# A selective-scan kernel: b made in quads of states, one more product on GpSimd, a second buffer for the inputs

## The chip, the cores and the metric

The kernel runs on one core of one Trainium2 chip. The metric is device time in microseconds (us) of one execution; lower is better. The core has five engines with instruction queues of their own, each worked off in order: TensorE (PE, matrix products), VectorE (DVE), ScalarE (ACT), GpSimd (POOL) and SyncE (SP), which here only issues transfers between DRAM and the core's memory.

## The reference

The input has shape (2, 96, 128, 128). Two layers follow one another, and only the first half of layer 0 is touched by the change: a normalization over the 96 channels, then a selective scan (Mamba) in four directions over the 16,384 positions (rows, rows backwards, columns, columns backwards), fused by one matrix.

```
xz = x @ in_w.T;  xc, z = split(xz)            # 192 channels each
xc = silu(causal_conv4(xc) + conv_b)
dt_raw, B, C = split(xc @ xproj_w.T)           # 6, 16, 16
dt = softplus(dt_raw @ dt_w.T + dt_b)
h[t] = exp(dt[t] * A) * h[t-1] + dt[t] * B[t] * xc[t]   # per channel and state
y[t] = sum over the 16 states of h[t] * C[t],  then + D * xc[t]
out = (y * silu(z)) @ outp_w.T                 # then the fuse matrix over the 4 directions
```

After it come two small feed-forward layers with 8-bit rounding and a 3x3 depthwise convolution; they are not changed.

## The kernel before, in words

For each of the two images three stages run one after the other: `normalize` writes the normalized image to DRAM once in rows (xnr) and once in columns (xnc); `mamba` does the scan; `ffn_and_conv` does the rest.

`mamba` handles two directions at once: 2 x 192 = 384 channels are three groups g = 0, 1, 2 of 128 partitions. Time is cut into 32 tiles of T = 512 positions; with two pairs of directions that makes 64 steps an image. A step has 24 units, each a group g and a pair of states s, s+1 (s = 0, 2, ..., 14); unit number = 8g + s/2. For each unit:

- `decay` (ScalarE) makes da = exp(dt * A), two rows of 512, in PSUM (three buffers).
- `b_part` (GpSimd) multiplies dtu = dt * xc into the row of B that a transfer has spread over all 128 partitions, 128 x 1024, in place (line 345); a small addition on column 0 brings in the state from the step before (line 347), in every step but the first of a pair of directions.
- `scan` (VectorE, line 357) runs the recurrence over 512 positions, once for each state, in place over da.
- VectorE multiplies h by the spread row of C (line 431, "the product"); TensorE adds the products of all states into y by matrix products with the identity (`sums`, line 361).
- For the units in `BY_POOL`, (0, 4) and (1, 4), that is units 2 and 10, GpSimd makes the product instead (`by_pool`, line 364); the scan then writes over b. `by_pool` is put into the order one unit later, its sum three units later.

B and C rows are fetched by SyncE for four states at a time, 1 MB each once spread (`row_tile`, line 341); B has four buffers (row0), C three (row1). A buffer of C is free again when TensorE has summed it. `fetch` asks for B six units ahead and for C four units ahead, both from even units.

The next step's preparation (`prologue`) is interleaved with the units: input projection and convolution as matrix products (`conv`, three of them, for g = 1, 0, 2, at units 1, 3, 5), SiLU on ScalarE (`silu`, which loads an activation table before and after), B, C and dt rows, softplus with three additions on GpSimd (`dt_q`, `dt_log`, `dt_sum`, lines 295, 298, 301) and dtu (`dt_u`, line 305). `load` fetches the two input tiles xa and xb (T + 3 columns each) two units before the step in which they are used.

The order on every engine is that in which the code issues the instructions; a table `todo` holds, for each unit and each half of it (0: before the scans, 1: after), what is to be issued there. The loop over units k:

```
for k in range(total + 6):
    ...
    if k % 2 == 0:
        fetch(k + 2 * B_AHEAD, 0, B_AHEAD, bs)
    feed(k + AHEAD)
    issue(k, 0)
    ... scan(0), behind(k - 1), feed_decay(k + AHEAD), scan(1)
    if k % 2 == 0:
        fetch(k + 2 * C_AHEAD, 1, C_AHEAD, cs)
    issue(k, 1)
```

`behind(k - 1)` issues the product of the unit before and its sums, so unit k's two scans stand around the product of unit k - 1. At a group's first unit it also issues the gating of the finished group (`gated`, line 368).

Of the kernel before, what the change touches and what calls it, by code (L numbers as in the profile page):

```python
# [10 lines left out]
F32 = mybir.dt.float32  # L11
# [4 lines left out]
ALU = mybir.AluOpType  # L16
# [7 lines left out]
T = 512  # L24
# [8 lines left out]
B_AHEAD = 3  # L33
C_AHEAD = 2
AHEAD = 2
BY_POOL = ((0, 4), (1, 4))
BCO = 32
NBC = 4 * S

# [2 lines left out]
def tile_metaformer(ctx: ExitStack, tc: tile.TileContext, a: dict, out: bass.AP):  # L42
    nc = tc.nc
# [135 lines left out]
    def mamba(acc, xnr, xnc):  # L179

        with ExitStack() as st:
            pool = lambda n, bufs, **kw: st.enter_context(tc.tile_pool(name=n, bufs=bufs, **kw))
            io, one, two, gen = pool("io", 1), pool("one", 1), pool("two", 2), pool("gen", 4)
            ps_w, ps_y, ps_m = (pool(n, k, space=PSUM) for n, k in (("ps_w", 3), ("ps_y", 1), ("ps_m", 1)))
            rows_d = pool("rows_d", 3, space=DRAM)

# [1 line left out]
            enter = one.tile([128, NG, S], F32, name="enter")  # L188
# [18 lines left out]
            def prologue(pi, i, d):  # L207
# [19 lines left out]
                def conv_out(g):  # L227
                    if g == 1:
                        d["xc"] = two.tile([128, NG, T], F32, name="xc")
                    t = mixed("xc") if g == 1 else d["xc"][:, g, :]  # L230
                    nc.scalar.activation(t, d["ps"], AF.Identity, bias=convb[:, pi, g : g + 1])  # L231
# [4 lines left out]
                def gate_out(g):  # L236
                    if g == 1:
                        d["sz"] = two.tile([128, NG, T], F32, name="sz")
                    nc.scalar.copy(mixed("sz") if g == 1 else d["sz"][:, g, :], d["ps"])

                def mixed(name):
                    d["mix", name] = one.tile([128, T], F32, name=f"mix_{name}")
                    return d["mix", name]

                def mix(name):
# [89 lines left out]
            def row_tile(d, g, s, k, ahead):  # L335

                t = gen.tile([128, 4, T], F32, name=f"row{k}", bufs=ahead + 1)

                src = d["bcd"][k, s // 4] if g == 1 else d["bcd"][k, s // 4, g // 2 : g // 2 + 1]
                n = src.shape[0]  # L340
                nc.sync.dma_start(t, src[None].broadcast_to((128 // n, n, 4, T)))
                return t

            def b_part(i, d, g, s, b):
                nc.gpsimd.tensor_tensor(b, d["dtu"][g][:, None, :].broadcast_to((128, 2, T)), b, ALU.mult)  # L345
                if i > 0:
                    nc.gpsimd.tensor_tensor(b[:, :, 0], b[:, :, 0], enter[:, g, s : s + 2], ALU.add)  # L347

            def decay(pi, d, g, s):

# [5 lines left out]
            def scan(j, da, b, h):  # L356
                nc.vector.tensor_tensor_scan(h[:, j, :], da[:, j, :], b[:, j, :], 0.0, ALU.mult, ALU.add)  # L357
# [29 lines left out]
            steps = [(pi, i) for pi in range(2) for i in range(NT)]  # L387
            units = [(g, s) for g in range(NG) for s in range(0, S, 2)]
            nu = len(units)
            total = nu * len(steps)  # L390
            state = [{} for _ in steps]
            todo = {}

            def later(k, where, f, *args):
                todo.setdefault((k, where), []).append(partial(f, *args))

            def issue(k, where):
                for f in todo.pop((k, where), ()):
                    f()

            for k, where, f in prologue(*steps[0], state[0]):
                if k < nu:
                    f()
                else:
                    later(k - nu, where, f)
            bs, cs, das, hs = {}, {}, {}, {}

            def fetch(k, n, ahead, m):
                if k < total:
                    t = row_tile(state[k // nu], *units[k % nu], n, ahead)  # L410
                    m[k], m[k + 1] = t[:, 0:2, :], t[:, 2:4, :]

            def feed(k):
                if k < total:
                    n = k // nu
                    b_part(steps[n][1], state[n], *units[k % nu], bs[k])

            def feed_decay(k):
                if k < total:
                    n = k // nu  # L420
                    das[k] = decay(steps[n][0], state[n], *units[k % nu])
# [3 lines left out]
            def behind(k):  # L425

                n, u = divmod(k, nu)
                (pi, i), d, (g, s) = steps[n], state[n], units[u]
                h, c = hs.pop(k), cs.pop(k)
                if (g, s) not in BY_POOL:  # L430
                    nc.vector.tensor_tensor(c, h, c, ALU.mult)  # L431
                nc.scalar.copy(hst[:, g, s : s + 2], h[:, :, T - 1])  # L432
                if s == 0:
                    if k > 0:
                        pn, pu = divmod(k - 1, nu)
                        gated(steps[pn][0], state[pn], units[pu][0], ys.pop(k - 1))
                    y = ps_y.tile([128, T], F32, name="y")
                    nc.tensor.matmul(y, dmat[:, pi, g, :], d["xc"][:, g, :], start=True, stop=False)  # L438
                else:
                    y = ys.pop(k - 1)  # L440
                ys[k] = y
                if (g, s) in BY_POOL:
                    later(k + 1, 1, by_pool, h, c)
                    later(k + 3, 1, sums, s, y, c)
                else:
                    sums(s, y, c)
                if k == total - 1:
                    gated(pi, d, g, y)
                if s == S - 2 and g > 0:
                    later(k + 3, 0, project, pi, i, d, g)  # L450
                    later(k + 3, 1, collect, pi, d, g)

            for m, (n, ahead) in ((bs, (0, B_AHEAD)), (cs, (1, C_AHEAD))):
                for k in range(ahead):
                    fetch(2 * k, n, ahead, m)
            for k in range(AHEAD):
                feed(k)
                feed_decay(k)
            for k in range(total + 6):
                n, u = divmod(k, nu)  # L460

                ahead = 1 if k == 0 else n + 2 if u == nu - 2 else len(steps)
                if ahead < len(steps):
                    for m, where, f in prologue(*steps[ahead], state[ahead]):
                        later(max(k, (ahead - 1) * nu + m), where, f)
                if k % 2 == 0:
                    fetch(k + 2 * B_AHEAD, 0, B_AHEAD, bs)
                feed(k + AHEAD)
                issue(k, 0)
                if k < total:  # L470
                    (g, s) = units[u]
                    da, b = das.pop(k), bs.pop(k)
                    hs[k] = b if (g, s) in BY_POOL else da
                    scan(0, da, b, hs[k])
                if 0 < k <= total:
                    behind(k - 1)
                feed_decay(k + AHEAD)
                if k < total:
                    scan(1, da, b, hs[k])
# [3 lines that stand above are left out]
# [102 lines left out]
    for b in range(NB):  # L585
        xnr = dpool.tile([C, L], F32, name="xnr")
        xnc = dpool.tile([C, L], F32, name="xnc")
        normalize(b, acc, xnr, xnc)
        mamba(acc, xnr, xnc)
        ffn_and_conv(b, acc)  # L590
# [71 lines left out]
```

## Time and profile before

| | before |
|---|---|
| device time, median of 3 | 12191.46 us (12177.44 to 12192.11) |
| profiled span | 12199.4 us |
| VectorE busy | 10961.9 us, 90% |
| TensorE busy | 10593.4 us, 87% |
| GpSimd busy | 10388.1 us, 85% |
| ScalarE busy | 8592.7 us, 70% |
| granted TensorE clock | 0.975 of full |

The scan stage takes from about 145 to 5530 us and again from about 6230 to 11620 us of the span; `normalize` and `ffn_and_conv` take the rest. Within the scan stage VectorE is busy 96% and GpSimd 95% (for example 482.5 and 477.6 us of the 500 between 1000 and 1500 us), and the transfers move some 313 GB/s. Busy time is the union of the recorded durations, and two instructions of VectorE overlap in the records by about 0.09 us: what counts for a sum is the distance from one start to the next, 1.12 us for a scan whose mean duration is 1.215. A group's row reads: line, engine, operation, what it writes and reads, shape, count, then busy time and mean of one in ns, then idle time before it and what ended it.

### The profile page before, as it was taken

The page shows a single profiled execution, that of the slowest core. Times are in us where ns is not written, and L with a number is a line of the kernel's source. Part 1 is how long each engine was busy: PE and PEld are TensorE (multiplying, and loading weights), DVE is VectorE, ACT ScalarE, POOL GpSimd, SP SyncE. Part 2 cuts the span into 40 slices and gives each one's busy share as a digit, 9 for nine tenths or more (in the row PEclk, how much of TensorE's full clock was granted, in tenths as well). Part 3 has the DMA queues.
Part 4 walks back from the last instruction along what each step waited for, and adds up shares of the span by engine and source line. Part 5 has one row for each costly group of instructions (what it writes and reads, how often), then busy time and mean ns, then how long its engine had stood idle before and what let it go on. Part 6 is the DMA issues. An engine that isn't in the chain of part 4 may idle for free. (4 is left out here: it accounts for less than half of the span.)

```text
span 12199.4 us, 100157 instructions
## 1 busy us (share of the span) xinstructions
PE 10593.4 (87%) x24208; PEld 4009.0 (33%) x24208; DVE 10961.9 (90%) x10624; ACT 8592.7 (70%) x15110; POOL 10388.1 (85%) x8360
## 2 busy tenths in 40 slices
PE   7888888888888888888978888888888888888889
PEld 2333333333333333333323333333333333333333
DVE  5999999999999999995469999999999999999954
ACT  6777777777777777765567777777777777777655
POOL 4999999999999999991159999999999999999911
PEclk8999999999999999999989999999999999999999
DMA  6887888888878878871068888878877878878700
GB/s 237 310 321 306 312 319 312 314 318 313 315 307 311 319 304 316 314 307 43 26 231 311 310 315 312 320 312 312 320 303 311 315 312 313 310 305 317 305 32 13
DMA packets 539204, 3417.36 MB, mean 280 GB/s; under 512 B 67276, under 2 KB 68396, under 8 KB 140696
## 3 DMA queue, kind: packets, MB, share of 16 engines
q1 hardware_dynamic: 538616, 3410.94, 72.5%
q8 instruction: 195, 3.19, 0.1%
q14 instruction: 393, 3.22, 0.1%
HBM read 3289.04 MB, written 54.53 MB: 274 GB/s over the span
## 5 line engine op out<-in xcount | busy, mean ns | idle before, releaser
L345 POOL TENSOR_TENSOR row<-dtu,row 128x1024 f32<-128x1024 f32 x3072 | 7235.6, 2356 | 262.2 <-DMA row<-bcd 212.3
L357 DVE TENSOR_TENSOR_SCAN da<-da,row 128x512 f32<-128x512 f32 x5632 | 6649.6, 1215 | 509.8 <-POOL row L347 166.1
L361 PE MATMUL y<-row,ident 128*128 128x512 f32 x12288 | 5956.1, 618 | 1135.8 <-DVE row L431 1131.4
L353 ACT ACTIVATE da<-dt,amat 128x512 f32<-128x512 f32 x6144 | 4249.9, 692 | 286.4 <-DVE row L357 99.3
L361 PEld LDWEIGHTS y<-row,ident 128*128 128x128 f32 x12288 | 2265.7, 193 | 4646.6 <-issue 2284.6
L431 DVE TENSOR_TENSOR row<-da,row 128x1024 f32<-128x1024 f32 x2816 | 3395.9, 1206 | 3.2 <-DMA row<-bcd 3.1
L432 ACT COPY hst<-da 128x2 f32<-128x2 f32 x2816 | 435.4, 155 | 1450.9 <-DVE row L431 1436.5
L204 PE MATMUL misc<-xa,inx 96*64 96x512 f32 (+1 forms) x2048 | 950.5, 607 | 133.1 <-DMA xa<-xnr 97.5
L556 POOL TENSOR_TENSOR acc<-acc,y 96x512 f32<-96x512 f32 x128 | 147.6, 1153 | 987.0 <-DVE y L555 972.6
L204 PE MATMUL misc<-xb,inx 96*64 96x512 f32 (+1 forms) x2048 | 949.7, 607 | 1.6 <-ACT xc L231 1.6
L347 POOL TENSOR_TENSOR row<-row,enter 128x2 f32<-128x2 f32 x2976 | 577.4, 194 | 233.4
L357 DVE TENSOR_TENSOR_SCAN row<-da,row 128x512 f32<-128x512 f32 x512 | 617.0, 1205 | 0.0
L364 POOL TENSOR_TENSOR row<-row,row 128x1024 f32<-128x1024 f32 x256 | 602.7, 2354 | 1.2 <-issue 0.6
L568 PE MATMUL pc<-pad,kw 96*96 96x512 f32 x1152 | 566.8, 593 | 0.0
L438 PE MATMUL y<-xc,dmat 128*128 128x512 f32 x768 | 432.1, 645 | 145.8 <-DVE sz L368 145.8
L295 POOL TENSOR_TENSOR q<-e,q 128x512 f32<-128x512 f32 x384 | 487.3, 1269 | 76.6 <-ACT q L292 71.5
L231 ACT ACTIVATE xc<-misc,convb 128x512 f32<-128x512 f32 x256 | 175.9, 687 | 525.8 <-PE misc L204 525.8
L204 PEld LDWEIGHTS misc<-xa,inx 96*64 96x64 f32 (+1 forms) x2048 | 326.8, 165 | 643.3 <-issue 470.1
L301 POOL TENSOR_TENSOR dt<-dt,ln 128x512 f32<-128x512 f32 x384 | 488.2, 1271 | 30.1
L298 POOL TENSOR_TENSOR ln<-ln,q 128x512 f32<-128x512 f32 x384 | 488.3, 1272 | 0.2
L305 POOL TENSOR_TENSOR dtu<-dt,xc 128x512 f32<-128x512 f32 x384 | 487.9, 1271 | 0.2
L378 PE MATMUL misc<-sz,gmat 128*96 128x512 f32 x1024 | 483.5, 594 | 0.0
(81 smaller groups left out, 9124.5 us busy)
## 6 DMA issues: line engine op xcount, KB each, us to landing
row<-bcd SPq DMA_DIRECT2D x3072, 1024.0 KB, 7.0
xc<-mix_xc SPq DMA_DIRECT2D x256, 128.0 KB, 5.3
sz<-mix_sz SPq DMA_DIRECT2D x256, 128.0 KB, 5.4
xa<-xnr SPq DMA_DIRECT2D x124, 193.1 KB, 5.3
xb<-xnc SPq DMA_DIRECT2D x124, 193.1 KB, 5.5
bcd<-rows SPq DMA_DIRECT2D x128, 128.0 KB, 6.5
acc<-in_x_dram SPq DMA_DIRECT2D x16, 768.0 KB, 8.6
xnr<-xn SPq DMA_DIRECT2D x16, 768.0 KB, 4.3
```

What stands on the lines that cost most here:

```text
L204: nc.tensor.matmul(ps[rows, :], w(PAIRS[pi][d], k, lo, hi), src[d][:, k : k + T], **se)
L298: nc.gpsimd.tensor_tensor(d["ln"], d["ln"], d["q"], ALU.add)
L301: nc.gpsimd.tensor_tensor(d["dt"][g], d["dt"][g], d["ln"], ALU.add)
L305: nc.gpsimd.tensor_tensor(dtu, d["dt"][g], d["xc"][:, g, :], ALU.mult)
L345: nc.gpsimd.tensor_tensor(b, d["dtu"][g][:, None, :].broadcast_to((128, 2, T)), b, ALU.mult)
L347: nc.gpsimd.tensor_tensor(b[:, :, 0], b[:, :, 0], enter[:, g, s : s + 2], ALU.add)
L353: nc.scalar.activation(da[:, j, :], d["dt"][g], AF.Exp, scale=amat[:, pi, g, s + j : s + j + 1])
L357: nc.vector.tensor_tensor_scan(h[:, j, :], da[:, j, :], b[:, j, :], 0.0, ALU.mult, ALU.add)
L361: nc.tensor.matmul(y, ident, c[:, j, :], start=False, stop=s + j == S - 1)
L364: nc.gpsimd.tensor_tensor(c, h, c, ALU.mult)
L431: nc.vector.tensor_tensor(c, h, c, ALU.mult)
L568: nc.tensor.matmul(pc, kw[:, t, :], rows, start=t == 0, stop=t == 8)
```

## The change

The change has four parts. GpSimd makes b for four states in one instruction of 128 x 2048 instead of two of 128 x 1024, and adds the entering state for four states at once; this is meant to save instructions on GpSimd. The room goes to a third product by GpSimd, (2, 4), which is unit 18; this takes a product from VectorE. The input tiles xa and xb get a second buffer; to make room in memory, the two tiles that hold xc and z of the mixed group before they are rearranged share one buffer. The preparation of step 1 is issued before the first fetches of rows and not in unit 0; for all later steps the preparation is registered at the same unit as before.

```diff
-BY_POOL = ((0, 4), (1, 4))
+BY_POOL = ((0, 4), (1, 4), (2, 4))
...
-            io, one, two, gen = pool("io", 1), pool("one", 1), pool("two", 2), pool("gen", 4)
+            io, one, two, gen = pool("io", 2), pool("one", 1), pool("two", 2), pool("gen", 4)
...
-                    d["mix", name] = one.tile([128, T], F32, name=f"mix_{name}")
+                    d["mix", name] = one.tile([128, T], F32, name="mix")
...
-                nc.gpsimd.tensor_tensor(b, d["dtu"][g][:, None, :].broadcast_to((128, 2, T)), b, ALU.mult)
+                nc.gpsimd.tensor_tensor(b, d["dtu"][g][:, None, :].broadcast_to((128, 4, T)), b, ALU.mult)
                 if i > 0:
-                    nc.gpsimd.tensor_tensor(b[:, :, 0], b[:, :, 0], enter[:, g, s : s + 2], ALU.add)
+                    nc.gpsimd.tensor_tensor(b[:, :, 0], b[:, :, 0], enter[:, g, s : s + 4], ALU.add)
...
+            def prepare(n):
+                if n < len(steps):
+                    for m, where, f in prologue(*steps[n], state[n]):
+                        k = (n - 1) * nu + m
+                        if k < 0:
+                            f()
+                        else:
+                            later(k, where, f)
+
+            prepare(1)
...
                     m[k], m[k + 1] = t[:, 0:2, :], t[:, 2:4, :]
+                    if n == 0:
+                        quads[k] = t
...
-                    b_part(steps[n][1], state[n], *units[k % nu], bs[k])
+                    b_part(steps[n][1], state[n], *units[k % nu], quads.pop(k))
...
+            feed(0)
             for k in range(AHEAD):
-                feed(k)
                 feed_decay(k)
...
-                ahead = 1 if k == 0 else n + 2 if u == nu - 2 else len(steps)
-                if ahead < len(steps):
-                    for m, where, f in prologue(*steps[ahead], state[ahead]):
-                        later(max(k, (ahead - 1) * nu + m), where, f)
+                if u == nu - 2:
+                    prepare(n + 2)
                 if k % 2 == 0:
                     fetch(k + 2 * B_AHEAD, 0, B_AHEAD, bs)
-                feed(k + AHEAD)
+                    feed(k + AHEAD)
```

GpSimd's order after the change, from unit 12's quad on, as the program has it: quad 12, product 10, quad 14, entering, quad 16, softplus of the next step's first group up to its sum, quad 18, dtu, quad 20, softplus of the second group up to its sum, product 18, quad 22, dtu, entering, quad 0 of the next step, dt_q, quad 2, dt_log, dt_sum, dtu, quad 4, product 2, quad 6, entering, quad 8, quad 10.

More of the change, by code (lines that the diff above doesn't have):

```diff
@@ L405, in mamba @@
                     later(k - nu, where, f)
-            bs, cs, das, hs = {}, {}, {}, {}
+            def prepare(n):
[7 more added lines that the diff above has]
+            prepare(1)
+            bs, cs, das, hs, quads = {}, {}, {}, {}, {}
             def fetch(k, n, ahead, m):
```

## The prediction

> **What bounds the kernel now.** I read the page first (shares, costliest groups), then the timeline of each engine over one step of the scan stage, then the list of waits, SyncE's own included. A step (512 columns of both directions) has 24 units, numbered 0 to 23, unit = 8g + s/2.
>
> ```profile
> PE 10593.4 (87%) x24208; PEld 4009.0 (33%) x24208; DVE 10961.9 (90%) x10624; ACT 8592.7 (70%) x15110; POOL 10388.1 (85%) x8360
> L345 POOL TENSOR_TENSOR row<-dtu,row 128x1024 f32<-128x1024 f32 x3072 | 7235.6, 2356 | 262.2 <-DMA row<-bcd 212.3
> L364 POOL TENSOR_TENSOR row<-row,row 128x1024 f32<-128x1024 f32 x256 | 602.7, 2354 | 1.2 <-issue 0.6
> L301 POOL TENSOR_TENSOR dt<-dt,ln 128x512 f32<-128x512 f32 x384 | 488.2, 1271 | 30.1
> ```
>
> Totals don't decide. Per step VectorE has 48 scans and 22 products at a pitch of 1.12 us (start to start) and 3 gatings at 0.60: 80.3 us. GpSimd has 24 b at 2.585 (2.36 + 0.08 before the small addition + 0.145 for it), 2 products at 2.33, three softplus chains of 5.03 and 3 x 0.18: 82.3. Yet a step takes 83.2 in half of the cases and 84.05 on average (end of the last product to the next such end, in the timeline, the 124 steps after the first of each batch). So I asked which chain closes the step. VectorE around one step (start, duration, [wait]):
>
> ```profile
> 2005.05 1.21 DVE L431 TENSOR_TENSOR row<-da,row 128x1024 f32<-128x1024 f32 x1
> ...
> 2036.45 1.23 DVE L357 TENSOR_TENSOR_SCAN da<-da,row 128x512 f32<-128x512 f32 x1 [0.68 <-ACT hst L432]
> 2037.59 1.21 DVE L431 TENSOR_TENSOR row<-da,row 128x1024 f32<-128x1024 f32 x1
> ...
> 2088.26 1.21 DVE L431 TENSOR_TENSOR row<-da,row 128x1024 f32<-128x1024 f32 x1
> ```
>
> The first and last are unit 23's product; call its end P (2006.26). The 0.68 is the wait before unit 9; from there to the next P (2089.47) VectorE has no gap. TensorE and ScalarE fill the stretch before it:
>
> ```profile
> 2006.31 1.98 PE L361 MATMUL y<-row,ident 128*128 128x512 f32 x4 [1.38 <-DVE row L431]
> 2008.23 0.64 PE L204 MATMUL misc<-xa,inx 96*64 96x512 f32 x1
> ...
> 2024.80 3.60 PE L204 MATMUL misc<-xb,inx 96*128 96x512 f32 x8
> 2028.24 8.75 PE L361 MATMUL y<-row,ident 128*128 128x512 f32 x20
> ```
> ```profile
> 2028.44 0.69 ACT L231 ACTIVATE xc<-misc,convb 128x512 f32<-128x512 f32 x1 [1.43 <-PE misc L204]
> ...
> 2030.65 1.28 ACT L251 ACT_TABLE_LOAD   x1
> 2031.94 1.48 ACT L251 ACTIVATE xc<-xc 128x1536 f32<-128x1536 f32 x1
> 2033.44 1.28 ACT L252 ACT_TABLE_LOAD   x1
> ...
> 2034.93 1.42 ACT L353 ACTIVATE da<-dt,amat 128x512 f32<-128x512 f32 x2
> ```
>
> TensorE sums unit 23, then runs without a gap through the next step's three convolutions; ScalarE takes the last one, does the SiLU with its two table loads, then the decay of unit 9, and VectorE starts unit 9 at P+30.19. This loop (TensorE, ScalarE, VectorE) is the 83.2. Where the step is longer, the convolution mostly began late, waiting for xa or xb.
>
> GpSimd stands in a second loop, just short of binding:
>
> ```profile
> 2038.33 0.20 POOL L347 TENSOR_TENSOR row<-row,enter 128x2 f32<-128x2 f32 x1
> 2039.26 2.35 POOL L345 TENSOR_TENSOR row<-dtu,row 128x1024 f32<-128x1024 f32 x1 [0.74 <-DMA row<-bcd]
> ```
> ```profile
> POOL row L345 <- DMA row<-bcd: 212.3, 104, 6.6
> SPq L341 <- PE y L361: 5297.7, 1518, 15.5
> ```
>
> SyncE issues in order, and mostly waits for TensorE to free a C buffer. C of units 8, 9 takes the buffer of units 2, 3, and unit 2 is one of GpSimd's products, summed late: in the middle of the x20 above, at 2031.8. SyncE issues at 2031.87, B of unit 12 behind it at P+26.2, landing at P+33.4. So GpSimd starts unit 12 at P+33.54 (median; mean 34.12). From there it has no gap until b of unit 23 is ready, 43.76 later; VectorE needs 5.69 from scan 23 to P. Together 33.54 + 49.45 = 83.0: 0.2 under the other loop, and in the slower steps over it.
>
> **What the Trainium skill says.** "GPSIMD Engine Reference", 3.1, gives 4497 ns for a two-input fp32 operation of 2048 elements. The trace agrees in slope: 1271 ns at 512 and 2356 at 1024 make 1085 per 512, hence 4.53 us at 2048, with 0.19 saved against two halves. The same page, 8, says that GpSimd shares its SBUF interfaces with VectorE when that has two SBUF inputs; here L345 stays between 2337 and 2380 ns beside a full VectorE, so I add nothing. "DMA: Bandwidth & Descriptors", Anatomy of one DMA, fits 2.0 us + bytes/436e3, an estimate of 4.4 us for 1 MB; here the median is 7.0, since transfers queue. "Perfetto Trace Analysis", Optimizing Scalar/DVE Operations, says that breaking up instructions may let others go on sooner; quads do the opposite. No run shows yet what that costs.
>
> **The change part by part.**
> *b by quads.* 24 pairs (2.585) become 12 quads: 4.53 + 0.08 + 0.145 = 4.755, so 0.415 saved per quad, 5.0 per step. But a quad is ready as a whole: its first unit waits 2.17 us longer than before.
> *Third product with C (unit 18).* VectorE loses 1.12, GpSimd gains 2.33. It is queued directly in front of the quad of units 22, 23.
> *Softplus.* With no b in odd units, three of its additions directly follow what they read: 3 x 0.09.
> GpSimd's total: 12 x 4.755 + 3 x 2.33 + 15.1 + 0.8 = 80.0, less than 82.3. VectorE: 79.2. On totals the change pays.
> *The chain from unit 12.* B of unit 12 still lands at P+33.4: TensorE's queue from P to unit 2's sum, and SyncE's order, don't change. From there to the end of the quad of 22, 23 GpSimd has six quads (28.53), two products (4.66), softplus of the first and second group up to its sum (2 x (1.225 + 0.09 + 1.345 + 1.235) = 7.79), one dtu (1.22), one entering (0.18): 42.4. Before, these products numbered one, and unit 23 was needed one unit (3.36) later. VectorE then needs from scan 22 to P eight operations, 7 x 1.12 + 1.21 = 9.06. Sum 51.5 against 49.45.
> So P to P is 33.54 + 51.5 = 85.0 in the median and 34.12 + 51.5 = 85.6 on average, while VectorE's loop would give 83.2 - 1.12 = 82.1. VectorE waits some 3 us before unit 22; GpSimd, done early with unit 10, idles some 5 us before unit 12. Further quads: unit 4 about 1.1 us late, unit 6 about 0.4, both hidden, since unit 9 waits for ScalarE anyway.
> *Late sum of unit 18.* C of unit 0 gets its buffer after that sum, some 5 us later in VectorE's work; SyncE has B of unit 4, C of unit 2 and xa, xb behind it. The 3 us wait of VectorE absorbs most of it, but xb, which lands 0.6 us before the convolution starts, may come up to 1 us later. I take 0.2 per step; 0 to 1 for the range.
> *Second input buffer.* The load stands at the same place of SyncE's queue in every later step, and its latency, not the old buffer, is what delays it: nothing. *Shared mix tile*: xc's and sz's uses are 11 units apart: nothing.
> *First load ahead of the row fetches.* In each batch's first step VectorE waits 9.7 us at unit 4 for ScalarE, behind a convolution whose inputs queued after seven row fetches. About 8 us a batch saved (0 to 12): -16.
> Sum: (85.6 + 0.2 - 84.05) x 126 = +220, - 16: 12191 + 204 = 12395 us.
>
> **Rivals.**
> *VectorE's loop sets the step* (14%): quads are early enough and each step loses the product: 12191 - 1.12 x 126 - 16 = 12034. For it: both totals fall. Against it: the 0.2 us of slack at unit 23.
> *Even* (9%): B of unit 12 lands earlier, or the quad costs 4.5 instead of 4.755 (six of them: 1.5 us), about 12200. Against it: the linear durations.
> *The burst delays the inputs* (12%): xb lands 2 us later and the whole TensorE chain with it, 87.3 a step: 12600. For it: 34 waits for xa exist already (69 us in all). Against it: VectorE's own wait spaces the transfers out.
> *GpSimd's chain from unit 12 binds* (65%): 12395.
>
> **How the numbers follow.** The forecast's own spread is +-100: the quad +-0.08 (six: 0.5 us, 60 us in all), the landing +-0.5. The range goes from just under the even case, 12170, to 12570. Faster: the first rival and a little of the second, 0.16; same 0.06; slower 0.78.
>
> **What would show it.** Right: quads of 4.5 us; GpSimd waiting for the B rows nearly every step, 4 to 5 us, at unit 12; a wait of about 3 us for GpSimd on VectorE before unit 22 and nowhere else of weight; steps of 85 to 86 us. Wrong: VectorE without a gap from unit 9 to 23, or GpSimd starting unit 12 before P+32; or steps over 87 with TensorE waiting for xa.

## The result and the profile after

| | before | after |
|---|---|---|
| device time, median | 12191.8 us | 12564.4 us (12541.8 to 12570.3) |
| ratio of after to before | | 1.0296, 95% interval 1.0281 to 1.0312 |
| mean step of the scan stage | 84.05 us | 87.18 us |
| granted TensorE clock | 0.975 | 0.956 |

The changed kernel is 373 us slower. Of the 23 runs of the kernel before that stand beside four of the experiments, one was slow (27041 us at a granted clock of 0.40) and is left out of every ratio. The page of the changed kernel, its first part and the rows of the groups that the change touches:

```profile
PE 10868.3 (86%) x24208; PEld 4137.5 (33%) x24208; DVE 10849.7 (86%) x10496; ACT 8547.8 (68%) x15110; POOL 10204.0 (81%) x5464
L345 POOL TENSOR_TENSOR row<-dtu,row 128x2048 f32<-128x2048 f32 x1536 | 6949.3, 4525 | 908.5 <-DMA row<-bcd 708.1
L364 POOL TENSOR_TENSOR row<-row,row 128x1024 f32<-128x1024 f32 x384 | 903.6, 2353 | 9.5 <-DVE row L357 5.4
```

Both engines that the change was to relieve did less: VectorE fell from 10961.9 to 10849.7 us and GpSimd from 10388.1 to 10204.0. The quad costs 4525 ns. What grew is waiting: GpSimd's idle time before b rose from 262.2 to 908.5 us, and three quarters of the rise is put down to B rows from DRAM (212.3 to 708.1 us).

One step shows where. In it P, the end of the product of unit 23, is 1885.68. GpSimd's timeline of the changed kernel (start, duration, what, idle time before it), from the quad of units 12 and 13 to that of units 22 and 23:

```profile
1920.50 4.52 POOL L345 TENSOR_TENSOR row<-dtu,row 128x2048 f32<-128x2048 f32 x1 [5.73 <-DMA row<-bcd]
...
1955.82 2.34 POOL L364 TENSOR_TENSOR row<-row,row 128x1024 f32<-128x1024 f32 x1
1958.13 4.53 POOL L345 TENSOR_TENSOR row<-dtu,row 128x2048 f32<-128x2048 f32 x1
1962.73 0.21 POOL L347 TENSOR_TENSOR row<-row,enter 128x4 f32<-128x4 f32 x1
```

The first line is quad 12 (units 12 and 13): GpSimd waited 5.73 us for its rows. From there GpSimd has no gap until 1962.94: 42.44 us. The second line is the new product of unit 18, directly in front of quad 22. VectorE meanwhile:

```profile
1959.20 1.22 DVE L357 TENSOR_TENSOR_SCAN da<-da,row 128x512 f32<-128x512 f32 x1
1962.97 1.23 DVE L357 TENSOR_TENSOR_SCAN da<-da,row 128x512 f32<-128x512 f32 x1 [2.56 <-POOL row L347]
```

It waits 2.56 us before unit 22, for exactly the small addition that ends quad 22. Then the end of the same step, SyncE's queue and TensorE:

```profile
1958.19 9.52 SPq L341 DMA_DIRECT2D row<-bcd  x4
1967.76 0.44 SPq L220 DMA_DIRECT2D xa<-xnr  x1
1968.25 0.43 SPq L220 DMA_DIRECT2D xb<-xnc  x1
```
```profile
1957.43 7.01 PE L361 MATMUL y<-row,ident 128*128 128x512 f32 x12
...
1972.11 1.98 PE L361 MATMUL y<-row,ident 128*128 128x512 f32 x4 [1.38 <-DVE row L445]
1976.91 1.04 PE L204 MATMUL misc<-xa,inx 96*64 96x512 f32 x2 [2.83 <-DMA xa<-xnr]
...
1978.54 1.06 PE L204 MATMUL misc<-xa,inx 96*64 96x512 f32 x1
```

The sum of unit 18 is the last in the x12, by the program's order, and ends at 1964.44. Of the four row fetches in SyncE's first line the last three start at 1964.47, 1964.90 and 1967.39, as the single records of the trace have it: C of unit 0, which needs the buffer that this sum frees, then B of unit 4 and C of unit 2, 3 MB asked for within 3 us, with xa and xb behind them. On average SyncE asks for C of unit 0 8.26 us before P, against 10.89 in the kernel before, in both 0.02 us after TensorE has freed the buffer. xb is there at 1977.54. TensorE, ready at 1974.1, waits 2.83 us, and then most of its first matrix products take 1.06 us each, where they took 0.59 to 0.64 before. The input tiles' own view says how often this happens. Before, and after:

```profile
  PE misc L204: 69.1, 34
```
```profile
  PE misc L204: 116.5, 90
```

TensorE waited for xa or xb 34 times before and 90 times after. So two things lengthen the step: the wait before unit 22, and inputs that come late.

### The profile page after: what moved, and what is told of

Read it like the earlier page. It is cut to its first block, busy times and chain, and to the rows that moved or that the text cites. A ratio compares the mean times of both kernels' runs of the same rounds, so it can differ in the third digit from the quotient of the medians.

```text
span 12568.5 us, 95842 instructions
## 1 busy us (share of the span) xinstructions
PE 10868.3 (86%) x24208; PEld 4137.5 (33%) x24208; DVE 10849.7 (86%) x10496; ACT 8547.8 (68%) x15110; POOL 10204.0 (81%) x5464
## 5 line engine op out<-in xcount | busy, mean ns | idle before, releaser
L345 POOL TENSOR_TENSOR row<-dtu,row 128x2048 f32<-128x2048 f32 x1536 | 6949.3, 4525 | 908.5 <-DMA row<-bcd 708.1
L357 DVE TENSOR_TENSOR_SCAN da<-da,row 128x512 f32<-128x512 f32 x5376 | 6383.9, 1216 | 996.6 <-POOL row L347 422.0
L361 PE MATMUL y<-row,ident 128*128 128x512 f32 x12288 | 6084.1, 632 | 979.9 <-DVE row L445 972.4
L361 PEld LDWEIGHTS y<-row,ident 128*128 128x128 f32 x12288 | 2350.3, 199 | 4567.0 <-issue 2463.3
L445 DVE TENSOR_TENSOR row<-da,row 128x1024 f32<-128x1024 f32 x2688 | 3240.4, 1206 | 0.1
L204 PE MATMUL misc<-xa,inx 96*64 96x512 f32 (+1 forms) x2048 | 987.3, 626 | 203.1 <-DMA xa<-xnr 171.9
L204 PE MATMUL misc<-xb,inx 96*64 96x512 f32 (+1 forms) x2048 | 984.3, 625 | 4.0 <-DMA xb<-xnc 2.0
L357 DVE TENSOR_TENSOR_SCAN row<-da,row 128x512 f32<-128x512 f32 x768 | 925.7, 1205 | 0.0
L364 POOL TENSOR_TENSOR row<-row,row 128x1024 f32<-128x1024 f32 x384 | 903.6, 2353 | 9.5 <-DVE row L357 5.4
L384 ACT COPY acc<-misc 96x512 f32<-96x512 f32 x192 | 172.7, 899 | 490.2 <-PE misc L378 490.2
```

Of the source, the lines that this page charges most:

```text
L204: nc.tensor.matmul(ps[rows, :], w(PAIRS[pi][d], k, lo, hi), src[d][:, k : k + T], **se)
L361: nc.tensor.matmul(y, ident, c[:, j, :], start=False, stop=s + j == S - 1)
L364: nc.gpsimd.tensor_tensor(c, h, c, ALU.mult)
```

## The experiments

Two theories of what costs the time, and a third part that they have to be told from. *Order*: the product of unit 18 stands in front of quad 22 and lengthens GpSimd's chain from unit 12. *Late inputs*: unit 18's sum comes late, so a C buffer comes free late, so fetches bunch up in front of xa and xb. *Quads*: b for four states is handed over later than b for two. In the expectations, theory A is *order*, with the late sum as its second part, rival L is *late inputs* alone and rival Q is *quads*. Every ratio is against the kernel before, run beside it on the same chip; the steps are taken from each trace as in the prediction. The kernel before itself had medians of 12192 us beside the changed kernel and 12195 to 12222 beside the experiments, so a difference in us between two versions is good to some 30 us where they did not run side by side.

**The third product taken away.** On the changed kernel:

```diff
-BY_POOL = ((0, 4), (1, 4), (2, 4))
+BY_POOL = ((0, 4), (1, 4))
```

> The changed kernel without the third product on GpSimd (unit 18); quads, second buffer and early first load stay. Theory A (the product queued in front of the last quad lengthens GpSimd's chain from unit 12, and its late sum delays the inputs): the wait before unit 22 goes, steps of 83.2 us in most cases, some 12150 us. Rival Q (the quads' late hand-over costs the time): still 12450 or more, with VectorE waiting for GpSimd before even units.

Measured: 12151 us, ratio 0.9949 (0.9930 to 0.9968); steps of 83.13 us in the median, mean 83.67; the wait before unit 22 is 0.06 us on average, where the changed kernel has 2.69. Quads, second buffer and early first load together are a small gain. The third product is what costs.

**The third product alone.** On the kernel before:

```diff
-BY_POOL = ((0, 4), (1, 4))
+BY_POOL = ((0, 4), (1, 4), (2, 4))
```

> The kernel before with the third product alone: pairs, one input buffer, first load where it was. Theory A: GpSimd's chain from unit 12 to the b of unit 23 is 43.8 + 2.3 = 46.1 us, so steps as in the changed kernel or longer, 12560 to 12650 us. Rival Q: VectorE loses 1.12 us in each step, about 12050 us.

Measured: 12595 us, ratio 1.0306 (1.0288 to 1.0325); steps of 87.24 us on average, VectorE waiting 2.16 us before unit 22 and 0.49 before 23. So the loss doesn't need quads: pairs suffer as much. This doesn't show that the late hand-over is free. By the prediction's figures the way from unit 12 to P is 42.4 + 9.06 = 51.5 us with quads, where GpSimd works less but VectorE needs it a unit earlier, and 46.1 + 5.69 = 51.8 with pairs; 51.6 and 51.7 were measured. What quads save on the one side they lose on the other.

**The product behind the quad.** On the changed kernel, only the place of GpSimd's product moves; its sum on TensorE stays where it is:

```diff
-                    later(k + 1, 1, by_pool, h, c)
+                    later(k + (2 if g == 2 else 1), 1, by_pool, h, c)
```

> The changed kernel with GpSimd's product of unit 18 issued one unit later, behind the quad of units 22 and 23; its sum stands where it stood. If the wait of VectorE before unit 22 is what costs the time, the wait goes and the step falls to about 83 to 84 us, 12050 to 12200 us. If the late sum of unit 18 (late C buffer, transfers in a burst, late xa and xb, rival L) costs as much, the sum comes some 3 us later still, TensorE waits for xa in nearly every step, and the time stays at 12550 or goes above 12700 us although VectorE no longer waits before unit 22.

Measured: 13172 us, ratio 1.0781 (1.0765 to 1.0798). The wait before unit 22 is down to 0.35 us, yet a step takes 92.01. VectorE at unit 22, and TensorE where the next step's convolution starts:

```profile
2062.44 1.23 DVE L357 TENSOR_TENSOR_SCAN da<-da,row 128x512 f32<-128x512 f32 x1 [0.34 <-POOL row L347]
```
```profile
2073.31 1.98 PE L361 MATMUL y<-row,ident 128*128 128x512 f32 x4 [1.73 <-DVE row L445]
2081.54 1.09 PE L204 MATMUL misc<-xa,inx 96*64 96x512 f32 x1 [6.24 <-DMA xa<-xnr]
2082.18 1.11 PE L204 MATMUL misc<-xb,inx 96*64 96x512 f32 x1
```

The later the sum, the later xa: four row fetches leave SyncE between 2066.14 and 2070.2 and xa stands behind them at 2070.26. The convolution starts 6.7 us after P on average (after: 3.2, before: 2.4). The late inputs are a cause of their own, and not a mark of the wait before unit 22. The product has also moved in front of quad 0 here, which the run "Both moves" takes apart.

**Inputs fetched earlier.** On the changed kernel the load moves from two units to eight units ahead of its step, which the second buffer allows:

```diff
-                at = [(-2, 1, load), (2, 1, partial(mix, "xc")), (6, 1, partial(silu, "xc"))]
+                at = [(-8, 1, load), (2, 1, partial(mix, "xc")), (6, 1, partial(silu, "xc"))]
...
-                if u == nu - 2:
+                if u == nu - 8:
```

> The changed kernel with xa and xb fetched 8 units before their step and not 2, which the second buffer allows. The waits of TensorE for xa go. Theory A with the inputs as second part: the step falls to what it is now where TensorE doesn't wait, 85.75 us, 12380 us, with 2.5 to 3 us of wait before unit 22 left. If the late inputs were only a symptom, the time stays within 30 us of 12564; if they were the whole cause, it falls to 12050.

Measured: 12324 us, ratio 1.0088 (1.0073 to 1.0104). No wait of TensorE for xa is left outside the two starts; the steps are 84.99 us in the median and 85.16 on average. What remains is the wait before unit 22, 2.83 us on average:

```profile
1929.09 1.23 DVE L357 TENSOR_TENSOR_SCAN da<-da,row 128x512 f32<-128x512 f32 x1 [2.21 <-POOL row L347]
```
```profile
1938.22 1.98 PE L361 MATMUL y<-row,ident 128*128 128x512 f32 x4 [1.13 <-DVE row L445]
1940.13 0.64 PE L204 MATMUL misc<-xa,inx 96*64 96x512 f32 x1
```

The convolution starts right behind the sum, at 0.64 us a product. The late inputs cost the changed kernel 12564 - 12324 = 240 us (about 250 by the ratios), and 56 us more than the expectation had, which took the steps without a wait for xa as its measure. The granted clock, 0.953 against 0.956, is no higher than in the changed kernel, so a lower mean clock is not by itself what costs these 240 us.

**Inputs earlier, without the third product.** First on the kernel before, with the second buffer, the shared mix tile and the same move of the load:

```diff
-            io, one, two, gen = pool("io", 1), pool("one", 1), pool("two", 2), pool("gen", 4)
+            io, one, two, gen = pool("io", 2), pool("one", 1), pool("two", 2), pool("gen", 4)
...
-                    d["mix", name] = one.tile([128, T], F32, name=f"mix_{name}")
+                    d["mix", name] = one.tile([128, T], F32, name="mix")
...
-                at = [(-2, 1, load), (2, 1, partial(mix, "xc")), (6, 1, partial(silu, "xc"))]
+                at = [(-8, 1, load), (2, 1, partial(mix, "xc")), (6, 1, partial(silu, "xc"))]
...
-                ahead = 1 if k == 0 else n + 2 if u == nu - 2 else len(steps)
+                ahead = 1 if k == 0 else n + 2 if u == nu - 8 else len(steps)
```

> The kernel before with the second input buffer (and the shared mix tile) and xa and xb fetched 8 units ahead; pairs, two products, first load where it was. If late inputs are what makes some of its steps longer than 83.2, steps fall from 84.05 to about 83.4 on average (GpSimd's chain still passes 83.2 in some), about 12110 us and no wait of TensorE for xa outside the first steps. If they are a symptom, 12190.

Measured: 12110 us, ratio 0.9916 (0.9883 to 0.9949).

Then on the changed kernel, the first edit of this section (two products) and the earlier load together:

```diff
-BY_POOL = ((0, 4), (1, 4), (2, 4))
+BY_POOL = ((0, 4), (1, 4))
...
-                at = [(-2, 1, load), (2, 1, partial(mix, "xc")), (6, 1, partial(silu, "xc"))]
+                at = [(-8, 1, load), (2, 1, partial(mix, "xc")), (6, 1, partial(silu, "xc"))]
...
-                if u == nu - 2:
+                if u == nu - 8:
```

> The changed kernel without the third product and with xa and xb fetched 8 units ahead. GpSimd's chain from unit 12 is 2.3 us shorter than in the changed kernel and ends under VectorE's loop, so every step is 83.1 to 83.2 us: 12050 to 12070 us. If quads alone bring time beyond the slack they give, it would fall under 12000.

Measured: 12077 us, ratio 0.9889 (0.9856 to 0.9922); steps of 83.13 us in the median, mean 83.21. Against this run the changed kernel with early inputs is 12324 - 12077 = 247 us longer, 2.0 us a step: that is the price of a third product in this place. The run is 7 us above its expected range. The two runs here differ by 32 us, some 26 of which the first load accounts for (last experiment): once the inputs are early, quads by themselves bring next to nothing. With quads GpSimd idles 5.4 us before unit 12 in every step.

**Both moves.** On the changed kernel, the product behind the quad and the inputs early:

```diff
-                at = [(-2, 1, load), (2, 1, partial(mix, "xc")), (6, 1, partial(silu, "xc"))]
+                at = [(-8, 1, load), (2, 1, partial(mix, "xc")), (6, 1, partial(silu, "xc"))]
...
-                    later(k + 1, 1, by_pool, h, c)
+                    later(k + (2 if g == 2 else 1), 1, by_pool, h, c)
...
-                if u == nu - 2:
+                if u == nu - 8:
```

> The run with the product of unit 18 behind the quad of 22 and 23 and, besides, xa and xb fetched 8 units ahead. If the late inputs alone made that run slow (rival L alone), steps fall to VectorE's loop less one product, 82 to 83 us, 11930 to 12060 us. If C of unit 0 itself comes too late, VectorE waits for it or for TensorE at units 0 to 4 and the step stays over 84 us, over 12200.

Measured: 12231 us, ratio 1.0015 (1.0005 to 1.0024), steps of 84.42 us. TensorE starts its convolution on time in every step; but VectorE at units 0 and 4:

```profile
1920.16 1.23 DVE L357 TENSOR_TENSOR_SCAN da<-da,row 128x512 f32<-128x512 f32 x1 [1.62 <-POOL row L347]
...
1934.80 1.23 DVE L357 TENSOR_TENSOR_SCAN da<-da,row 128x512 f32<-128x512 f32 x1 [1.46 <-POOL row L347]
```

The wait has moved, as the numbers for a step over 84 us had it, but what it is for was neither C nor TensorE: it is GpSimd's quad 0, in front of which the product now stands. Behind one quad is in front of the next, and GpSimd has no gap from quad 12 to past quad 4. Its product and quad 0:

```profile
1913.01 2.35 POOL L364 TENSOR_TENSOR row<-row,row 128x1024 f32<-128x1024 f32 x1
1915.31 4.53 POOL L345 TENSOR_TENSOR row<-dtu,row 128x2048 f32<-128x2048 f32 x1
```

Against the run with the late inputs (13172 us) the early load alone is worth 941 us.

**The product where GpSimd waits.** By the order on GpSimd the product of unit 8 stands directly in front of quad 12, in the gap; inputs early:

```diff
-BY_POOL = ((0, 4), (1, 4), (2, 4))
+BY_POOL = ((0, 4), (1, 0), (1, 4))
...
-                at = [(-2, 1, load), (2, 1, partial(mix, "xc")), (6, 1, partial(silu, "xc"))]
+                at = [(-8, 1, load), (2, 1, partial(mix, "xc")), (6, 1, partial(silu, "xc"))]
...
-                if u == nu - 2:
+                if u == nu - 8:
```

> The changed kernel with GpSimd's third product moved from unit 18 to unit 8, where its order puts it directly in front of the quad of units 12 and 13, that is into the 5 us in which GpSimd waits for that quad's B rows; xa and xb fetched 8 units ahead. Theory A (what counts is where in the order the product stands, not how many there are): GpSimd's chain from unit 12 ends at 33.5 + 49.1 = 82.6, VectorE's loop at 82.1, steps of 82.6 to 83.0, 11980 to 12040 us. If GpSimd's total or a third late sum is what hurts, as slow as with unit 18, 12320.

Measured: 12041 us, ratio 0.9860 (0.9827 to 0.9892), 1.4% faster than the kernel before, and the fastest version here, 1 us above its expected range. Steps are 82.88 us in the median and 82.89 on average. GpSimd around quad 12:

```profile
1923.69 0.20 POOL L347 TENSOR_TENSOR row<-row,enter 128x4 f32<-128x4 f32 x1
1926.19 2.36 POOL L364 TENSOR_TENSOR row<-row,row 128x1024 f32<-128x1024 f32 x1 [2.30 <-DMA row<-bcd]
1928.55 4.52 POOL L345 TENSOR_TENSOR row<-dtu,row 128x2048 f32<-128x2048 f32 x1
```

The product fills the second half of the gap, and quad 12 starts at P + 33.2 as it did without it. With the same count of products as the changed kernel, the same quads and GpSimd as full as ever, no wait before unit 22 is left. It misses 82.6 because of another wait, which the product brought along:

```profile
1925.15 1.42 ACT L353 ACTIVATE da<-dt,amat 128x512 f32<-128x512 f32 x2 [0.91 <-DVE row L357]
```

ScalarE's decay for unit 9 starts when the second scan of unit 8, which now writes over b, has ended; without the product in this place it had no such wait. Why the new place brings it was not tested. VectorE reaches unit 9 at P + 30.99, against 30.11 in the run with two products and early inputs.

**The buffers and the first load alone.** On the kernel before, the second input buffer, the shared mix tile and the first load in front of the row fetches:

```diff
-            io, one, two, gen = pool("io", 1), pool("one", 1), pool("two", 2), pool("gen", 4)
+            io, one, two, gen = pool("io", 2), pool("one", 1), pool("two", 2), pool("gen", 4)
...
-                    d["mix", name] = one.tile([128, T], F32, name=f"mix_{name}")
+                    d["mix", name] = one.tile([128, T], F32, name="mix")
...
+            for m, where, f in prologue(*steps[1], state[1]):
+                if m < 0:
+                    f()
+                else:
+                    later(m, where, f)
...
-                ahead = 1 if k == 0 else n + 2 if u == nu - 2 else len(steps)
+                ahead = n + 2 if u == nu - 2 else len(steps)
```

> The kernel before with the third and fourth part of the change alone: second input buffer, shared mix tile, first load in front of the first row fetches; pairs and two products stay. The forecast of these parts: nothing in later steps, since the load stands where it stood and its latency is what delays it; the first step of each batch shorter by 8 to 13 us (96.1 and 95.3 us before), so 16 to 26 us in all, some 12170 us. If the second buffer by itself helped the inputs, waits of TensorE for xa would go and the time fall to 12110.

Measured: 12170 us, ratio 0.9977 (0.9970 to 0.9984), 26 us less than the kernel before beside it. The first steps take 82.7 and 82.6 us instead of 96.1 and 95.3; the later ones average 84.07, as before (84.05), and TensorE still waits for xa 21 times (35 before, counted the same way). So the second buffer brings nothing that can be measured as long as the load stands where it stood.

## Why the prediction was right, and where its size was off

It said slower, 12395 us, with a range to 12570; the time is 12564. The direction and the main mechanism, GpSimd's chain from unit 12, are confirmed. The size is not: that the time lies 6 us inside the range is owed in part to luck, and it is nearer to the rival with late inputs (12600 us, given 12%) than to the forecast. One of the prediction's own signs of being wrong, steps over 87 us with TensorE waiting for xa, came true (87.18 us, 90 waits), together with the signs of being right: both mechanisms are at work at once, where the prediction let them compete. By its steps:

- *The quad's cost*: 4.53 us worked out, 4525 ns measured. Right.
- *GpSimd's chain from unit 12*: 42.4 us worked out, 42.44 in the step shown. From the start of quad 12 to P 51.5 worked out, 87.18 - 35.56 = 51.6 measured on average. Right.
- *The waits*: some 3 us before unit 22 (2.69 on average), some 5 us of GpSimd before unit 12 (5.98), and smaller ones at units 4 and 6, hidden because unit 9 waits for ScalarE anyway (0.59 us, as before). The first two are right, and so is that the others are hidden. As to their size, 1.1 us at unit 4 and 0.4 at unit 6 were forecast, and 1.15, 1.21 and 1.37 measured at units 4, 5 and 6; but the kernel before already had 1.00, 0.42 and 0.95 there, and in the changed kernel those at units 5 and 6 are put down to ScalarE. The match at unit 4 is no support for the reasoning on quads.
- *Quads' late hand-over*: counted as part of the chain, with no wait of its own; the third product alone on pairs, whose chain is as long, costs as much. Right.
- *Nothing added for sharing with VectorE*: the durations bear it out (4525 and 2353 ns). They don't test what the prediction cites of a VectorE with two inputs in SBUF, since VectorE's scans and products here have one of their inputs, da, in PSUM.
- *Buffer and mix tile nothing, first load 16 us*: 26 us by itself. Right in kind.
- *Late sum of unit 18*: this is the term that was mis-sized. The prediction took 0.2 us a step, 0 to 1 for the range. The start of quad 12 after P moved from 34.12 to 35.56 us, 1.44 a step, 181 us over 126 steps. The forecast had 25 of them, and the other 156 are nearly all of the 169 us that it lacks. With early inputs the start is at 33.43, so the late inputs account for all of it. The chain of events was named (C of unit 0, then B of unit 4, C of unit 2, xa and xb); what was wrong was the belief that VectorE's own wait would space the fetches out. C of unit 0 and C of unit 2 left 4.3 us apart on average, against 6.2 before, and xb landed 1.5 us later after P (3.76 against 2.26). The 0.6 us that xb was said to have in hand was read from one undisturbed step; on average before the change, xb landed 0.3 us after TensorE was ready for it. The prediction also counted only the later start. The convolution began 0.78 us later on average than before, but the C row of unit 8 was asked for 1.48 us later (27.83 against 26.35 after P): the convolution's first sixteen products took 4.67 us instead of 3.97, and some 0.25 of the difference is an effect of waiting on TensorE's speed, told in the last section.

The experiments add what the prediction couldn't tell apart: against quads with two products and early inputs, 247 us come from the product's place and, on top, 240 us from the late inputs; the changed kernel is 373 us and not 487 us over the kernel before because early inputs alone are worth 82 us there (98 against the runs beside it), the first load 26, and the quads a few.

## What to carry to other kernels

On an engine that works its queue in order, ask of a piece of work that is moved there not what it adds to the total but what stands behind it and who waits for that. The same 2.3 us cost 247 us in front of the last quad and brought a gain of 36 us (12077 to 12041) where GpSimd was waiting for rows anyway, though GpSimd's total was the same (10206 and 10209 us busy). A result that comes late also holds its buffer longer: follow the buffer to the fetch that needs it, and on to everything queued behind that fetch; a second buffer for a late input helps only when the load is also issued earlier.

## What the runs showed of the hardware that was not expected

A wait of TensorE can cost more than its own length. Where the convolution started without waiting for its inputs (86 steps of the kernel before) its first sixteen products took 3.7 us; after waits of up to 1.5 us (77 steps of the changed kernel) they took 4.3, at the same 0.6 us a product (xb lands 0.8 us behind xa on average there, which may be the reason); after waits of 2 to 3 us (21 steps of the changed kernel) they took 6.1. In 18 of these 21, products of about 1.06 us instead of 0.59 stand as in the timeline above; in that timeline the granted clock between 1979 and 1981 us was 0.50. In the changed kernel no wait under 1.8 us was followed by such products, and every one of the 15 over 2.5 us was. The Trainium skill, "TensorE: Matmul & The Clock Gate", What's actually happening, has TensorE fall to half its clock after one idle window of about 3.4 us; the trace agrees with the half, but here a wait of 2.83 us, after two of 1.38 and one of 0.93 within the 12 us before it, was enough.
